# The last attention of a four-layer block: side work cut into smaller pieces over more steps, and its transfers in another order

## The chip, the cores and the metric

The kernel runs on one core of a Trainium2 chip. A core has five engines that each follow their own program: PE (matmuls, with PEld for the loading of weights), DVE (vector work), ACT (activations and copies), POOL (elementwise work on data outside PSUM) and SP, which here only issues DMA transfers. The metric is the device time of one execution in microseconds (us): 1222.36 us, the median of three runs (1219.72 to 1225.01).

## The reference

Four layers update `x` (4 sequences of 1024 tokens, 256 channels), each as `x + tanh(gate) * layer(layernorm(x))`: a cross-attention to 77 context tokens, a mixture of six experts, a second cross-attention with 16 heads, and a self-attention, which this text is about:

```python
qkv = (x @ W_qkv).reshape(Bx, Nx, 3, H, D)          # H = 16 heads of D = 16
q, k, v = (qkv[:, :, 0], qkv[:, :, 1], qkv[:, :, 2])
...
pos = sim > 0.9                                      # a class for each token but the first 5
logits = jnp.einsum('bqhd,bkhd->bhqk', q * scale, k)
...
x_pos = masked_attn(pos)                             # keys: the 5 registers and the tokens of pos
x_neg = masked_attn(~pos)                            # keys: the 5 registers and the others
reg_out = (x_pos[:, :REG] + x_neg[:, :REG]) * 0.5
tok_out = jnp.where(pos[:, :, None, None], x_pos[:, REG:], x_neg[:, REG:])
out = jnp.concatenate([reg_out, tok_out], axis=1).reshape(Bx, Nx, Cx)
return out @ W_proj + b_proj
```

A token attends to the registers and to its own class. The five registers (the first five tokens of a sequence) attend twice, once to each class, and take the mean.

## The kernel before

Three layers and the projections of the last one are laid out by a planner (class `Plan`, with costs and due times), which ends about 435 us into the span. The projections store the last layer's queries, keys and values in DRAM (`q_d`, `k_d`, `v_d`). The change touches almost only what follows.

**Units and steps.** The last attention works in 16 units: sequence `b` (4) by group `g` of four heads. A unit's queries and keys are fetched into a slot (`QT`, `KT`, four slots, reused every fourth unit) by `fetch` (L193, twelve DMAs of 128 KB, issued at L206); `classes` (L1473) adds four DMAs with rows that hold the class as large numbers. A unit takes 16 steps: two halves `ch` of the queries by eight tiles `t` of the keys. Step `k` is step `k % 16` of unit `k // 16`, so 256 steps in all, after 11 steps (`LEAD`) in which only maxima are made. In a step the loop at L1898 issues, in program order on PE, DVE and ACT:

- `scores` (L1678): for each of four heads a matmul (L1682, keys by queries, 512 columns) into a bank `sc`, and ACT's exp of it into `p` (L1690);
- between them `maxima` (L1638) for the unit 11 steps ahead: a matmul (L1647, queries by keys) into a bank `ps_m`, and DVE's maximum of it (L1654);
- `weigh` (L1694): the `p` of the step before times the values (L1700, eight instructions for four heads), into a bank `av`; ACT copies it to `part` (L1717) and POOL adds it to `raw` (L1718). Once no maxima are left, DVE adds it directly (L1712).

There are eight PSUM banks, taken in turn. `maxima_end` (L1656) turns eight tiles' maxima, and four small DMAs (L1670) write them as rows of `QT`; no score of that half of the unit may start before they have landed. They are issued at steps `16u - 3` and `16u + 5`, for use from `16u` and `16u + 8`.

**Side work.** The rest is written as generators. `plan(steps, gen)` (L1855) names the steps at whose end a generator goes on to its next `yield`:

- `registers(b)` (L1561): POOL prepares the registers' queries (32 small products, L1568 and L1569), PE makes their scores (L1577, two banks of 512 columns with eight matmuls each), ACT copies them to `p_r` (L1584), then maximum, exp, transposes (L1598), weighting (L1605) and the registers' result. It runs at steps `64b + 16` to `64b + 26`.
- `finish(b)` (L1730), for the sequence before: reciprocals of the softmax sums (L1735), the sums to DRAM (L1737), two fetches of 512 KB that spread them over the partitions (`rinv`, L1739 and L1743, one buffer), a product of 128x1024 on POOL after each (L1741, L1745), then four output tiles: eight passes of matmul into one bank (L1755), DVE's sum of 512 columns (L1757), a DMA of the result (L1758).
- `finish_unit`, `first_heads`, `divided` and `last_heads` do the same for the last sequence in parts; `biased(b)` (L1839) adds the bias to `X[b]` on POOL; `unit(u)` (L1843) fetches a unit; `fetch_values(b)` (L1465) fetches V; `values(b)` (L1488) makes V for sequences 2 and 3 in the first steps.

**Queues.** The program order of PE, DVE, ACT and POOL is kept as written (`manual_schedule`). SP isn't in that list: the builder's scheduler orders SP's DMAs by when it reckons their inputs ready, with program order as the priority. Each queue then runs in its order, and an instruction that waits holds those behind it.

## Time and profile before

| | us |
|---|---|
| median of the three runs | 1222.36 |
| the profiled execution | 1224.2 |
| its span, first to last instruction | 1222.2 |
| first step of maxima (L1647) | 435.8 |
| step 0 (first exp of L1690) | 472.9 |
| steps 16 / 64 / 128 / 192 | 521.3 / 648.3 / 833.7 / 1018.3 |
| end of the loop's last exp step (255) | about 1209 |

Over the span PE is busy 1153.5 us (94%), DVE 991.2 (81%), ACT 928.1 (76%), POOL 603.8 (49%). The mean granted clock of PE is 0.968 of full speed. The costliest groups are all of the last attention: DVE's 1024 maxima (L1654), 623.1 us; ACT's 1024 exps (L1690), 545.6; PE's matmuls of L1647, L1700 and L1682; POOL's 213 sums (L1718), 272.2.

How to read it: a step begins with the first of its four exps, so the distance between the first exps of two steps is the first one's length. The table of windows gives, for any stretch, how long each engine was busy in it. In a timeline, the bracket at a line's end says how long the engine stood idle before it and what ended that; "<-issue" means that the profile shows no cause. SP's lines are only the issuing of DMAs; the data lands later.

### The profile page before, as it was taken

The numbers are of one execution on the slowest core, as the hardware profiler recorded it, in microseconds if no ns is written. First come the engines' busy times: TensorE is split into PE (matmuls) and PEld (weight loads), VectorE is DVE, ScalarE is ACT, GpSimd is POOL, SyncE is SP. The second block draws the span as 40 slices with busy tenths as digits, with TensorE's granted clock in tenths as the row PEclk, the third lists the DMA queues.
The fourth block names the chain that finished last, engine by engine and source line by source line (L and its number), as shares of the span: only waits on it lengthen the run. The fifth ranks groups of instructions, "written<-read, shape, count | busy, mean of one in ns | idle before, by whom it ended". The sixth has DMA issues, their size and how long they took to land.

```text
span 1222.2 us, 25427 instructions
## 1 busy us (share of the span) xinstructions
PE 1153.5 (94%) x9100; PEld 609.7 (50%) x9100; DVE 991.2 (81%) x2057; ACT 928.1 (76%) x1910; POOL 603.8 (49%) x670
## 2 busy tenths in 40 slices
PE   7999999999999979999998899999899999799998
PEld 5666776777676554344333354333354333244333
DVE  6898686776864379979999779999779999678983
ACT  4865567776566314989998779999778999678985
POOL 6463566667757531545444435444445444345431
PEclk8998999999999978999999899999899999899999
DMA  8000021111112877522232323332423332310001
GB/s 234 23 1 12 13 71 63 44 42 47 55 44 98 239 190 169 93 49 46 49 57 56 85 68 59 50 57 47 92 56 64 54 60 41 64 33 22 20 20 36
DMA packets 58149, 80.08 MB, mean 66 GB/s; under 512 B 15845, under 2 KB 41360, under 8 KB 58022
## 3 DMA queue, kind: packets, MB, share of 16 engines
q1 hardware_dynamic: 56406, 77.17, 27.6%
q8 instruction: 72, 1.18, 0.4%
q10 hardware_dynamic: 1104, 1.04, 0.3%
q0 software_dynamic: 512, 0.25, 0.2%
q14 instruction: 55, 0.45, 0.1%
HBM read 47.39 MB, written 26.07 MB: 60 GB/s over the span
## 4 chain that ended last, share of the span: by engine, by line
PE 55%; DVE 29%; DMA 5%; ACT 4%; issue 3%; POOL 3%; SPq 1%; DVEq 0%; POOLq 0%; ACTq 0%
DVE nm L1654 21%; PE av L1700 12%; PE sc L1682 11%; PE ps_m L1647 4%; PE ps_st L1120 4%; PE ps_av L1132 2%; PE ps_o L1198 2%; PE ps_q L1233 2%; PE ps_o L1755 2%; PE ps_xt L780 2%; ACT p L1690 2%; PE ps_y L989 2%; PE ps_rs L1577 1%; DMA k_d<-stage 1%; DMA slot<-nmt 1%
## 5 line engine op out<-in xcount | busy, mean ns | idle before, releaser
L1654 DVE TENSOR_REDUCE nm<-ps_m 128x1 f32<-128x512 f32 x1024 | 623.1, 675 | 54.3 <-PE ps_m L1647 45.5
L1690 ACT ACTIVATE p<-sc 128x512 f32<-128x512 f32 x1024 | 545.6, 672 | 61.9 <-PE ps_m L1647 53.5
L1718 POOL TENSOR_TENSOR raw<-raw,part 128x512 f32<-128x512 f32 x213 | 272.2, 1278 | 384.2 <-ACT part L1717 377.5
L1647 PE MATMUL ps_m<-slot,slot 64*128 64x512 f32 x768 | 286.2, 456 | 0.7
L1700 PE MATMUL av<-p,v 128*32 128x512 f32 x2048 | 280.0, 616 | 1.0
L1682 PE MATMUL sc<-slot,slot 64*128 64x512 f32 x768 | 249.0, 438 | 8.1 <-DMA slot<-nmt 7.7
L1682 PEld LDWEIGHTS sc<-slot,slot 64*128 64x128 f32 x768 | 124.1, 185 | 182.1 <-DVE nm L1654 76.8
L1717 ACT COPY part<-av 128x512 f32<-128x512 f32 x213 | 138.7, 651 | 18.2 <-PE av L1700 17.0
L1647 PEld LDWEIGHTS ps_m<-slot,slot 64*128 64x128 f32 x768 | 130.5, 187 | 27.1 <-ACT p L1690 13.3
L1682 PE MATMUL sc<-qt,kt 64*128 64x512 f32 x256 | 89.1, 457 | 24.7 <-issue 15.4
L1279 POOL TENSOR_TENSOR ss_all<-ss_all,mhalf 128x16 f32<-128x16 f32 x32 | 92.6, 2902 | 12.8 <-DVE ss_all L1250 12.8
L1647 PE MATMUL ps_m<-kt,qt 64*128 64x512 f32 x256 | 92.4, 465 | 4.1 <-ACT vs L1499 2.4
L1682 PEld LDWEIGHTS sc<-qt,kt 64*128 64x128 f32 x256 | 45.9, 198 | 88.7 <-DVE nm L1654 38.8
L1700 PEld LDWEIGHTS av<-p,v 128*32 128x32 f32 x2048 | 41.2, 109 | 81.6 <-ACT p L1690 66.6
L1125 ACT ACTIVATE pt<-ps_st 77x512 f32<-77x512 f32 x128 | 64.1, 598 | 22.8 <-PE ps_st L1120 22.8
L1068 DVE TENSOR_REDUCE nm<-ps_e 128x4 f32<-128x308 f32 x128 | 51.7, 469 | 13.7 <-PE ps_e L1055 13.6
L768 ACT ACTIVATE xnp<-x,shift_all,rstd_all 128x256 f32<-128x256 f32 x96 | 52.0, 605 | 11.7 <-POOL shift_all L747 9.3
L735 DVE BATCH_NORM_STATS2 bn_st<-x 128x6 f32<-128x256 f32 x128 | 51.6, 403 | 2.4 <-DMA x<-in_x 1.9
L1647 PEld LDWEIGHTS ps_m<-kt,qt 64*128 64x128 f32 x256 | 42.5, 191 | 18.3 <-DVE nm L1654 4.9
L670 DVE TENSOR_TENSOR stage<-ps_s,stage 128x512 fp32r<-128x512 f32 x32 | 22.0, 690 | 25.3 <-ACT stage L237 25.1
L237 ACT COPY xt<-ps_xt 128x512 f32<-128x512 f32 (+1 forms) x57 | 31.7, 582 | 13.9 <-PE ps_xt L780 13.4
L744 POOL TENSOR_SCALAR rstd_all<-mv_all 128x2 f32<-128x2 f32 (+3 forms) x46 | 11.7, 254 | 61.2 <-DVE mv_all L736 49.6
(323 smaller groups left out, 1658.1 us busy)
## 6 DMA issues: line engine op xcount, KB each, us to landing
slot<-q_d SPq DMA_DIRECT2D x72, 128.0 KB
slot<-k_d SPq DMA_DIRECT2D x72, 128.0 KB
q_d<-stage SPq DMA_DIRECT2D x32, 256.0 KB
k_d<-stage SPq DMA_DIRECT2D x16, 512.0 KB
v_d<-vs SPq DMA_DIRECT2D x16, 272.0 KB
v<-v_d SPq DMA_DIRECT2D x16, 272.0 KB
x<-in_x SPq DMA_DIRECT2D x8, 512.0 KB
rin<-inv_d SPq DMA_DIRECT2D x32, 128.0 KB
```

The source lines that it names most:

```text
L735: ve.bn_stats(st[:, i, :], X[b][:, t0 + i, :])
L768: se.activation(to[:, i, :], xb[:, t0 + i, :], AF.Identity, bias=shift[:, i : i + 1], scale=rstd[:, i : i + 1],)
L1068: ve.tensor_reduce(g2["nm"][:, i, r], by_head, AX.X, ALU.max, negate=True)
L1125: se.activation(p[:, r], g2["st", c][r], AF.Exp)
L1279: gp.tensor_tensor(ss, ss, mhalf.to_broadcast([P, H]), ALU.pow)
L1647: pe.matmul(ps, QT[u % SLOTS][r, i, t * P : t * P + P], KT[u % SLOTS][r, i, h * CH : h * CH + CH], start=True, stop=True,)
L1654: ve.tensor_reduce(nm[:, 2 * i + j // 2, t % (T // 2), h : h + 1], ps, AX.X, ALU.max, negate=True)
L1682: pe.matmul(ps, KT[u % SLOTS][r, i, t * P : t * P + P], QT[u % SLOTS][r, i, ch * CH : ch * CH + CH], start=True, stop=True,)
L1690: se.activation(p[j], ps, AF.Exp)
L1700: pe.matmul(ps[32 * j : 32 * j + 32, :], V_all[b % 2][:, at : at + 32], p[j], start=True, stop=True)
L1717: se.copy(part, ps)
L1718: gp.tensor_tensor(to, to, part, ALU.add)
```

## The change

It touches the last attention and one store ahead of it.

- The generator `fetch` yields after each half of the queries and of the keys (three DMAs), `classes` after each of its two tensors. A unit's fetches are written at steps `16u - 42` to `16u - 39` (`16u - 34` to `16u - 31` for the first unit of a sequence), its classes at `+8, +9` (`+4, +5`) after the first; before, all stood at `16u - 40`. Unit 1 and the V of sequence 0 move from ahead of the loop into its first steps. V of the others is fetched in two pairs.
- Both stores of the class rows go out on ACT's queue.
- `plan` takes a step in brackets, `(k,)`: the generator then goes on in the middle of step `k`, after two of its four heads. `filled(k)` names the end of step `k` and the middle of step `k + 1`: matmuls are issued at the one, their bank is emptied at the other.
- The registers' scores take four banks of 256 columns instead of two of 512, one every second step, emptied in mid-step. The rest of `registers` follows a few steps later.
- The output tiles of `finish` cover 128 tokens instead of 256, one every third step from `64b + 97`, with DVE's sum in mid-step; before, they stood at `64b + 81` to `64b + 89`. `first_heads` is cut in the same way.
- `finish` fetches both `rinv` at step `64b + 74`, into two buffers; before, the first at 69 and the second at 74 into the same buffer.
- `biased` adds the bias in four parts. `finish_unit(0)` ends at step 226 instead of 219. `on` shares the three buffers of `part`.

```diff
     def fetch(u, q_rows, k_rows):
...
                     nc.sync.dma_start(out=dst[to : to + D].bitcast(F32), in_=heads[:, k])
+                yield
...
-                for s_, queue in enumerate((nc.sync, nc.scalar)):
-                    queue.dma_start(out=cls_d[s_].rearrange("k (t n) -> t k n", n=P), in_=r[:, s_])
+                for s_ in range(2):
+                    nc.scalar.dma_start(out=cls_d[s_].rearrange("k (t n) -> t k n", n=P), in_=r[:, s_])
...
         blank(1)
         gp.memset(V_all[0][:, NV:], 0.0)
-        fetch(1, QT[1], KT[1])
-        classes(1)
-        drain(fetch_values(0))
...
-        yield
-
-        p = work.tile([P, S], F32, name="p_r", tag="rinv", bufs=1)
-        for h in range(2):
-            ps = bank("ps_rs", [P, CH])
-            for n in range(2 * G):
-                g, i = divmod(n, 2)
+            if g % 2:
+                yield
+
+        p = work.tile([P, S], F32, name="p_r", tag="rinv", bufs=2)
+        n = CH // 2
+        for h in range(4):
+            ps = bank("ps_rs", [P, n])
+            for k in range(2 * G):
+                g, i = divmod(k, 2)
...
-            se.copy(p[:, h * CH : h * CH + CH], ps)
-        yield
+            yield
+            se.copy(p[:, h * n : h * n + n], ps)
+            yield
...
+        rinv = [work.tile([P, S], F32, name="rinv", tag="rinv", bufs=2) for e in range(2)]
+        for e in range(2):
+            nc.sync.dma_start(out=rinv[e], in_=bc(rinv_d[b][8 * e : 8 * e + 8], 1, D))
+        yield
+        for e in range(2):
+            gp.tensor_tensor(o[:, e, :], o[:, e, :], rinv[e], ALU.mult)
+            if e == 0:
                 yield
...
+        for t in range(T):
+            ps = bank("ps_o", [P, C])
+            for e in range(2):
+                pe.matmul(ps, o[:, e, t * P : t * P + P], w_proj[:, e, :], start=e == 0, stop=e == 1)
             yield
+            ve.scalar_tensor_tensor(x[:, t, :], ps, tg[:, 3:4], x[:, t, :], ALU.mult, ALU.add)
+            yield
+            if t % 2:
+                at = (t - 1) * P
+                nc.sync.dma_start(
+                    out=out[b, at : at + 2 * P].rearrange("(t p) c -> p t c", p=P), in_=x[:, t - 1 : t + 1, :]
+                )
+            yield
...
+        for t in range(T):
+            ps = bank("ps_o", [P, C])
+            pe.matmul(ps, o[:, 0, t * P : t * P + P], w_proj[:, 0, :], start=True, stop=True)
+            yield
+            ve.scalar_tensor_tensor(x[:, t, :], ps, tg[:, 3:4], x[:, t, :], ALU.mult, ALU.add)
             yield
...
-        on = work.tile([P, n, P], F32, name="on", bufs=2)
+        on = work.tile([P, n, P], F32, name="on", tag="part", bufs=3)
...
+        for t in range(0, T, 2):
+            x2 = X[b][:, t : t + 2, :]
+            gp.tensor_tensor(x2, x2, bc(b_proj, 1, 2), ALU.add)
+            yield
...
-            plan([k - 24, k - 22, k - 20, k - 18], fetch_values(b))
+        plan([k - 40, k - 38, k - 16, k - 14] if b else [-5, -4, -2, -1], fetch_values(b))
+        scored = [filled(k + n) for n in (17, 19, 21, 23)]
+        plan([k + 14, k + 15, *chain(*scored), k + 25, k + 26, k + 27, k + 29, k + 30, k + 31], registers(b))
+        plan([k + 27, k + 28, k + 35, k + 36], biased(b))
+        if b < B - 1:
+            tiles = chain(*([n, (n + 1,), n + 2] for n in range(k + 64 + 33, k + 64 + 55, 3)))
+            plan([k + 67, k + 68, k + 74, k + 78, k + 80, *tiles], finish(b))
         else:
-            plan([k + 19, k + 27], finish_unit(0))
+            plan([k + 19, k + 34], finish_unit(0))
             plan([k + 35, k + 39], finish_unit(1))
-            plan([k + 43, k + 45, k + 47, k + 49], first_heads())
+            plan(chain(*(filled(k + n) for n in (41, 42, 43, 45, 46, 47, 49, 50))), first_heads())
+    for u in range(1, NU):
+        at = {1: -11, 2: -1}.get(u, 16 * u - (42 if u % G else 34))
+        plan([at, at + 1, at + 2, at + 3], rows_ := unit(u))
+        plan({1: [-7, -6], 2: [3, 4]}.get(u, [at + 8, at + 9] if u % G else [at + 4, at + 5]), rows_)
...
                 maxima(um, km, [(j + 2) % J])
+                if j == 1:
+                    for gen in middle.pop(k, []):
+                        next(gen, None)
```

## The prediction

> **What bounds the kernel now.** I began with the page's slices of the span, then cut the last attention (435.8 us to the end) into its units with a table of windows, and then followed the two bad kinds of unit in the timelines.
>
> ```profile
> DVE  6898686776864379979999779999779999678983
> ACT  4865567776566314989998779999778999678985
> ```
>
> From slice 16 on, DVE and ACT stand at 9 together, with dips that return every fifth or sixth slice. In the windows the columns are stretch, its length, then busy time (and count) of PE, PEld, DVE, ACT and POOL, the granted clock, the DMA engines' share and GB/s.
>
> ```profile
> 521.30:568.80 47.50, 47.23 (x358) 21.21 (x358) 41.69 (x74) 43.01 (x87) 22.98 (x30) 0.96 0.29 49
> 608.50:648.30 39.80, 39.73 (x262) 15.54 (x258) 39.66 (x71) 39.40 (x81) 17.89 (x14) 1.00 0.30 51
> 648.30:698.60 50.30, 42.43 (x262) 16.98 (x258) 40.74 (x73) 40.03 (x81) 20.18 (x15) 0.90 0.35 66
> 668.00:676.00 8.00, 0.55 (x6) 0.19 (x2) 1.68 (x3) 1.08 (x2) 1.26 (x1) 0.74 0.91 130
> 676.00:681.00 5.00, 4.62 (x20) 2.07 (x22) 2.20 (x4) 2.45 (x5) 0.26 (x1) 0.50 0.44 92
> 698.60:754.00 55.40, 54.72 (x390) 26.49 (x386) 44.91 (x80) 43.81 (x87) 26.24 (x33) 1.00 0.33 73
> 1068.20:1126.40 58.20, 55.65 (x390) 26.32 (x386) 46.48 (x80) 44.52 (x87) 29.18 (x36) 1.00 0.10 29
> ```
>
> A quiet unit of 16 steps (608.5) takes 39.8 us, with DVE and ACT both busy for over 39 of it: 2.45 us a step in the mean, 2.39 in the shortest. So whatever adds work to DVE or ACT, or holds PE long enough to starve them, is paid. The other units are longer for two reasons. In 648.3 (steps 64 to 79) DVE and ACT have no more work than in the quiet unit; they wait. In 698.6 (steps 80 to 95) there is real work: 128 more matmuls.
>
> **The wait.** SP's timeline around step 72 (start, length of the issues, line):
>
> ```profile
> 663.88 0.34 SPq L1737 DMA_DIRECT2D rinv_d<-sums  x1
> 664.32 1.84 SPq L1670 DMA_DIRECT2D qt<-nmt  x3
> 666.27 0.63 SPq L1739 DMA_DIRECT2D rinv<-rinv_d  x1
> 666.95 0.53 SPq L1670 DMA_DIRECT2D qt<-nmt  x1
> ...
> 667.97 8.23 SPq L206 DMA_DIRECT2D slot<-k_d  x6
> 676.30 2.23 SPq L1479 DMA_DIRECT2D slot<-cls_d  x4
> 689.82 0.64 SPq L1743 DMA_DIRECT2D rinv<-rinv_d  x1
> ```
>
> The fourth `nmt` row, without which no score of step 72 may start, goes out behind a `rinv` fetch of 512 KB, and the fetches of unit 7 follow at once. PE takes up the scores only at 676.38, after 7.83 us of waiting; the first exp of step 73 starts 11.98 us after that of step 72. Steps 136 and 200 repeat it with 11.76 and 12.10. Afterwards PE runs at half clock for 5 us (the window 676). The three units with this wait (50.3, 49.6, 49.9) exceed 39.8 by 30.4 us in all. The waits of SP's queue say the same from its side, and that the second `rinv` fetch held it once more, because its only buffer had to be multiplied out first:
>
> ```profile
> SPq L1743 <- POOL o L1741: 10.9, 1, 10.9
> ...
> SPq L206 <- DMA rinv<-rinv_d: 5.6, 1, 5.6
> ```
>
> A smaller wait of this kind stands at step 16: unit 3's fetches and classes are issued from 503.2 to 514.8, `nmt` from 515.64, and PE waits 5.03 us. Steps 15 and 16 take 6.38 and 3.82 (clock 0.66 again) in place of 2.45 each: 5.3 us.
>
> **The change, part by part.** All terms are against the profiled execution: 1224.2 us, of which the span is 1222.2; the median of the runs shown is 1.8 lower.
>
> Order of the transfers. The reciprocals come at steps 67 and 68, and the `rinv` transfers move to step 74, both into buffers of their own: behind the `nmt` of step 69, ahead of that of step 77, which step 80 needs. From 74 to 80 there are six steps, 14.7 us. By then must have landed: the rest of unit 7's fetches (12 of 128 KB, now from step 70; at the 130 GB/s of the window 668:676 they take 12 us from step 70, so until 75), the 64 KB of `rinv_d`, then 1 MB of `rinv`, about 8 us at that rate: to step 79. It fits, barely. I count 27 of the 30.4 us as gained, leaving about 1 us a place for what is late next: `nmt` behind `rinv` at step 80, or POOL's first product at 78 (2.38 us) with eight small register products of 0.2 us beside it; POOL is half idle in the quiet unit (17.89 of 39.8), and three `part` buffers cover some two steps. Unit 3's fetches move from step 8 to 6 to 9 and its classes behind the `nmt` of 13: 4.5 of 5.3 us. Both class stores on ACT's queue: one issue more of 0.35 us where ACT waits 3.17 us; nothing. The earlier fetches of unit 1 and of V move past the stores of `vs`, while DVE reduces without a gap from 450.6 to 465: nothing, with 3 us either way.
>
> The price of a small insert. `ps_ra` and today's tile give it:
>
> ```profile
> 549.74 1.08 PE L1605 MATMUL ps_ra<-v,pt_r 128*32 128x64 f32 x64
> ...
> 551.27 1.09 ACT L1690 ACTIVATE p<-sc 128x512 f32<-128x512 f32 x2 [0.52 <-PE ps_m L1647]
> ...
> 715.97 0.75 DVE L1757 SCALAR_TENSOR_TENSOR x<-ps_o,tg,x 128x512 f32<-128x512 f32 x1 [1.22 <-PE ps_o L1755]
> ```
>
> `ps_ra` delays the next score by 0.97 us (549.77 to 550.74); ACT idles 0.52, DVE is not the one that suffers, and the step costs 0.74 more than 2.39. An output tile of today (eight passes from 713.93, the next score at 715.86) delays it by 1.93: ACT idles 1.56, DVE 1.22, since its sum is queued ahead of the reductions and PE has not finished. So the first half microsecond is hidden by work in the banks, and the rest is paid.
>
> Registers' scores. Today 16 matmuls of 512 columns at 0.233 us hold PE from 529.18 to 533.09, DVE idles 3.72, the step takes 6.20: 3.8 us a batch. After: four pieces of eight matmuls with 256 columns. The trace has no such matmul. From below it is half of 0.233, so 0.93 us a piece (the transposes at 541.33 show weights changed every 0.11 us, so loading does not forbid it); from above the full 0.233, 1.86 a piece. I take 0.93, nearest to `ps_ra`. ACT pays 0.52 for it and about 0.28 for the copy of 256 columns (512 cost 0.48 from start to start), now emptied between two exps so that it waits for nothing: 0.8 a piece, 3.2 a batch, a gain of 0.6, in four batches 2.4. Bounds: 0.3 a piece (only the copy) and 1.7.
>
> Output tiles. The unit 698.6 exceeds the quiet one by 15.6; the register work alone costs 6.3 (47.5 of unit 521.3, less 39.8, less 1.4 of clock after step 16), so four tiles cost 9.3. In unit 1068.2 it is 18.4 less 6.3, 12.1, with about 1.5 of `finish_unit`. After: eight tiles with four passes of 0.217 (0.87), and a DVE sum of 256 columns, about 0.75 less 0.27 of columns, some 0.41 from start to start, after two reductions. Bounds 0.41 (DVE alone) and 1.0 (the doubled `first_heads` tiles of today, four passes and a wide sum, cost 0.9 to 1.3 at steps 235 to 241). I take 0.7, next to `ps_ra`'s 0.74: 5.6 a batch. Gains 3.7, 3.7 and 5.0: 12.4. They no longer share steps with the registers, so POOL's wait at step 81 goes too.
>
> `first_heads`: four tiles at 4.1 today, eight of two passes at 0.45: gain 0.5. The bias in pieces of 1.28 us in place of 4.57 on POOL, and the third `on` buffer: nothing, as POOL has room.
>
> Sum: 27 + 4.5 + 2.4 + 12.4 + 0.5 = 46.8; 1224.2 - 46.8 = 1177.
>
> The rule that speaks against it. In the unit 698.6 the clock stayed at 1.00 among inserts and waits up to 2 us. The Trainium skill, "TensorE: Matmul & The Clock Gate", section "A second HAM failure mode: psum-queue depth-cycling", warns that short idles between groups of matmuls that cycle through PSUM banks make the clock fall back and recover. By the page, if each of the 48 new pieces cost one window of 3.4 us at half speed, that would be an estimated 82 us, and the change a loss. The measured 1.00 speaks against it here, and the sum goes by the row.
>
> **The rivals.** (1) The wait moves: `nmt` of steps 77, 141, 205 lands behind both `rinv`, 4 to 5 us late each; for it, the tight count above and that one `rinv` with fetches beside it took until 676; 1191. (2) The change doesn't do what it says. SP's queue isn't in program order: the four V fetches of the second batch, written at steps 40 to 46, are issued at 494.01, in step 6. If the builder draws both `rinv` forward to step 69, ahead of `nmt`, the wait stays whole: 1177 + 27 = 1204. (3) Slower: a bank held from the step's end to the next step's middle leaves seven for the pipeline. PE waits for banks all the time (115.6 us of the scores' idle is for DVE's reductions). If each of the 48 pieces then costs two reductions of 0.6 beside its 0.93 and 0.28, 2.4 us, that is 115 us against the 48 of today's blocks: with the 31.5 of waits gone, 1224 + 35 = 1259. It decides from 1.7 us a piece; `ps_ra` with 0.74 in one bank speaks against.
>
> **Numbers.** Forecast 0.66, (1) 0.13, (2) 0.11, (3) 0.06; 0.04 that the parts cancel. The range runs from 1162, with the pieces near their lower bounds (tiles at 0.41, scores at 0.3: 15 us better), to 1204. Half a per cent, about 6 us, is what a measurement can tell: faster 0.90, same 0.04, slower 0.06.
>
> **What to look for.** Step 72 near 2.5 us with no wait for `nmt`, no half clock after it; steps 15 and 16 the same. A step with a piece near 3.1. Wrong would be a score that waits for `nmt` at step 80, ACT's `part` waiting for POOL at 79 to 82, or pieces above 1.2 us.

## The result, and the profile after

The change makes no gain: 1226.74 us, the median of 20 runs (1222.08 to 1231.06), beside 1222.96 for the kernel before on the same chip (20 runs, 1218.99 to 1225.98). The ratio is 1.0033, 95% interval 1.0020 to 1.0045: slower, by less than half a per cent. The profiled execution took 1226.41, its span 1224.7. The forecast was 1177.

The slices of the span, DVE and ACT, as shown of before:

```profile
DVE  5898786776864489889999699999689899689884
ACT  4766567876566327899999698899699899689676
```

The dips are still there: each now reaches 6 (before, two of the three stood at 7), and they have moved a little. The windows say where to. Columns as before: stretch, length, busy time (and count) of PE, PEld, DVE, ACT and POOL, granted clock, DMA share, GB/s.

```profile
599.40:639.20 39.80, 39.74 (x262) 15.54 (x258) 39.66 (x71) 39.42 (x82) 17.92 (x14) 1.00 0.39 65
639.20:681.70 42.50, 41.61 (x256) 15.90 (x254) 41.46 (x73) 40.00 (x81) 17.91 (x14) 1.00 0.34 52
681.70:738.60 56.90, 48.25 (x372) 23.07 (x373) 42.30 (x75) 43.42 (x90) 28.45 (x36) 0.94 0.29 60
738.60:784.50 45.90, 45.85 (x282) 18.56 (x279) 42.20 (x77) 40.49 (x80) 20.38 (x16) 1.00 0.33 58
1117.10:1173.70 56.60, 52.38 (x292) 22.25 (x291) 49.66 (x83) 41.52 (x82) 26.01 (x23) 0.94 0.08 21
...
671.00:677.00 6.00, 5.99 (x40) 2.88 (x40) 5.93 (x13) 6.00 (x13) 2.72 (x3) 1.00 0.01 1
680.00:688.00 8.00, 1.50 (x10) 0.34 (x10) 2.44 (x5) 2.40 (x5) 3.19 (x3) 0.90 0.50 127
```

The first row is a quiet unit, as long as before. Unit 4 (639.2) has lost its wait: 42.5 instead of 50.3. Unit 5 (681.7) has got one: PE is busy for 48.25 of 56.90, and in 680 to 688 nearly every engine stands while 127 GB/s come in. From 671 to 677 the DMA engines were idle. SP's timeline says why:

```profile
655.64 2.39 SPq L1672 DMA_DIRECT2D qt<-nmt  x4
658.08 2.26 SPq L206 DMA_DIRECT2D slot<-q_d  x5
660.38 3.43 SPq L206 DMA_DIRECT2D slot<-k_d  x6
664.53 0.34 SPq L1738 DMA_DIRECT2D rinv_d<-sums  x1
676.77 1.72 SPq L1672 DMA_DIRECT2D slot<-nmt  x3
678.59 1.33 SPq L1741 DMA_DIRECT2D rinv<-rinv_d  x2
679.97 0.56 SPq L1672 DMA_DIRECT2D slot<-nmt  x1
```

`rinv_d` went out at 664.5, and nothing followed for 12 us. In the queue's order both `rinv` stand behind three of the four `nmt` (the small DMAs of `maxima_end`) of step 77, though the program writes them at step 74; those `nmt` can't go out before DVE has made them, at 676.8. The fourth `nmt` then lies behind 1 MB. It is the picture of before, eight steps later and with twice the bytes. PE's timeline, and the page's group of score matmuls, before and after:

```profile
690.11 0.76 PE L1684 MATMUL sc<-slot,slot 64*128 64x512 f32 x1 [8.62 <-DMA slot<-nmt]
```

```profile
L1682 PE MATMUL sc<-slot,slot 64*128 64x512 f32 x768 | 249.0, 438 | 8.1 <-DMA slot<-nmt 7.7
L1684 PE MATMUL sc<-slot,slot 64*128 64x512 f32 x768 | 248.3, 440 | 29.8 <-DMA slot<-nmt 28.7
```

The span by stretches (starts of steps are first exps), so that the difference of 2.5 us is accounted for:

| stretch | before | after | difference |
|---|---|---|---|
| up to step 0 | 472.9 | 466.8 | -6.1 |
| unit 0 (steps 15 and 16: 10.2, then 8.1) | 48.4 | 44.5 | -4.0 |
| units 1, 2, 3 | 127.1 | 127.9 | +0.9 |
| units 4, 8, 12: steps 72, 136, 200 | 35.8 | 8.3 | -27.6 |
| the same units, other steps | 114.0 | 119.5 | +5.5 |
| units 5, 9, 13: steps 80, 144, 208 | 7.2 | 37.9 | +30.7 |
| the same units, other steps (tiles gone) | 161.8 | 134.0 | -27.8 |
| units 6, 7, 10, 11 (tiles come) | 159.3 | 178.3 | +19.0 |
| unit 14 | 44.7 | 56.6 | +11.9 |
| unit 15 and the end | 51.0 | 51.0 | 0 |

### The profile page after: what moved, and what is told of

It reads as the page before. It is cut to its first block, busy times and chain, and to the rows that moved or that the text cites. A ratio compares the mean times of both kernels' runs of the same rounds, so it can differ in the third digit from the quotient of the medians.

```text
span 1224.7 us, 25560 instructions
## 1 busy us (share of the span) xinstructions
PE 1157.0 (94%) x9164; PEld 611.3 (50%) x9164; DVE 999.4 (82%) x2073; ACT 932.1 (76%) x1918; POOL 607.0 (50%) x682
## 4 chain that ended last, share of the span: by engine, by line
PE 75%; DVE 11%; DMA 5%; ACT 4%; POOL 2%; issue 1%; SPq 0%; ACTq 0%; DVEq 0%; POOLq 0%
PE av L1702 20%; PE sc L1684 18%; PE ps_m L1649 8%; DVE nm L1656 5%; PE ps_st L1121 4%; DMA slot<-nmt 3%; PE ps_av L1133 2%; PE ps_o L1199 2%; PE ps_o L1755 2%; PE ps_q L1234 2%; PE ps_xt L781 2%; PE ps_y L990 2%; PE ps_rs L1578 1%; ACT p L1692 1%; PE ps_xb L886 1%
## 5 line engine op out<-in xcount | busy, mean ns | idle before, releaser
L1684 PE MATMUL sc<-slot,slot 64*128 64x512 f32 x768 | 248.3, 440 | 29.8 <-DMA slot<-nmt 28.7
L1684 PEld LDWEIGHTS sc<-qt,kt 64*128 64x128 f32 x256 | 43.0, 186 | 67.7 <-DVE nm L1656 31.4
L746 POOL TENSOR_TENSOR rstd_all<-rstd_all,mhalf 128x2 f32<-128x2 f32 (+3 forms) x46 | 39.5, 858 | 3.8
```

The lines of the kernel that those rows point to most:

```text
L1684: pe.matmul(ps, KT[u % SLOTS][r, i, t * P : t * P + P], QT[u % SLOTS][r, i, ch * CH : ch * CH + CH], start=True, stop=True,)
```

## The experiments

All times are medians beside runs of the kernel before on the same chip (1220.7 to 1221.0 in these comparisons), so the ratio to before is what compares them; after itself stands at 1.0033. L numbers are those of each kernel.

| run | us | ratio to before, 95% |
|---|---|---|
| rinv_step72 | 1202.24 | 0.9846 (0.9826 to 0.9866) |
| rinv_step70 | 1200.24 | 0.9833 (0.9812 to 0.9854) |
| rinv_late | 1207.93 | 0.9893 (0.9870 to 0.9916) |
| empty_at_once | 1211.88 | 0.9931 (0.9911 to 0.9950) |
| tiles_whole | 1224.41 | 1.0024 (1.0007 to 1.0041) |
| scores_whole | 1224.66 | 1.0034 (1.0020 to 1.0048) |
| bias_early | 1221.94 | 1.0010 (0.9994 to 1.0026) |
| recip_apart | 1226.07 | 1.0043 (1.0028 to 1.0057) |
| recip_later | 1223.41 | 1.0013 (0.9995 to 1.0031) |
| early_fetch | 1224.77 | 1.0036 (1.0021 to 1.0051) |
| before_late | 1198.80 | 0.9818 (0.9798 to 0.9838) |
| all_mended | 1192.81 | 0.9773 (0.9736 to 0.9810) |
| mended_step70 | 1182.37 | 0.9682 (0.9647 to 0.9717) |
| mended_step71 | 1199.69 | 0.9837 (0.9795 to 0.9879) |

**The place of the 1 MB in SP's queue.** My theory after the result: the order alone costs 30 us. The rival: the bytes don't fit between the two `nmt` in any order.

```diff
-            plan([k + 67, k + 68, k + 74, k + 78, k + 80, *tiles], finish(b))
+            plan([k + 67, k + 68, k + 72, k + 78, k + 80, *tiles], finish(b))
```

> The kernel after with one number changed: the three transfers of a finished batch (rinv_d, two rinv) are issued at step 72 of their unit instead of 74. In the order of SP's queue both rinv then stand ahead of all four nmt of step 77, with one k_d fetch between rinv_d and rinv and five k_d fetches behind. Theory (order in the queue): after lost 9.9 us at each of steps 80, 144 and 208 because the 1 MB started only behind three nmt that are issued at step 77, 7 to 8 us after rinv_d had landed; now it starts at about step 74, the nmt follow the fetches, and steps 80/144/208 fall from 12.4, 12.5 and 13.0 us to about 2.6: minus 30 us, 1197. Rival (the bytes): 1 MB and twelve fetches do not fit between step 70 and step 80 on the 16 engines in any order; the five k_d pushed behind the 1 MB hold the nmt, and step 80 stays 4 to 6 us too long, in all minus 12 to 18 us, 1209 to 1215. Second rival (the wait goes back to step 72): SP stands before rinv until rinv_d has landed and what is behind it comes late; then a wait of some us at step 72 to 76 or at unit 6's first step, and no gain.

SP's timeline of this run:

```profile
658.09 0.42 SPq L1738 DMA_DIRECT2D rinv_d<-sums  x1
658.56 0.43 SPq L206 DMA_DIRECT2D slot<-k_d  x1
663.28 1.34 SPq L1741 DMA_DIRECT2D rinv<-rinv_d  x2
664.68 2.32 SPq L206 DMA_DIRECT2D slot<-k_d  x5
674.48 4.83 SPq L1672 DMA_DIRECT2D slot<-nmt  x4
```

Two steps earlier in the program, and the 1 MB starts 15.3 us earlier (663.28 instead of 678.59; 13.0 counted from the start of step 72), ahead of all four `nmt`. The ratio falls from 1.0033 to 0.9846, some 23 us. It is not 30: steps 79 to 81 still sum to 13.0, 11.8 and 9.9 in place of some 8. SP's waits show why. It stood before `rinv` for some 4 us a batch until `rinv_d` had landed:

```profile
SPq L1741 <- DMA rinv_d<-sums: 12.5, 3, 4.3
```

And of the four `nmt`, which DVE had made by 674.8, the third went out only at 677.86, when the second `rinv` had landed; so the four took 4.83 us to issue instead of some 2.3. With step 70:

```diff
-            plan([k + 67, k + 68, k + 74, k + 78, k + 80, *tiles], finish(b))
+            plan([k + 67, k + 68, k + 70, k + 78, k + 80, *tiles], finish(b))
```

> The kernel after with the three transfers of a finished batch issued at step 70 of their unit instead of 74: rinv_d ahead of the first q_d fetch, both rinv behind the four nmt of step 69 and ahead of the other eleven fetches. With the transfers at step 72 the profile showed rinv waiting in SP's queue from 659.0 to 663.3 us for rinv_d, the DMA engines nearly idle from 662.3 to 665, both rinv and the fetches done at about 682, and the score of step 80 3.5, 2.4 and 1.5 us late in the three batches, with another 0.3 to 1.2 us in the step after. Theory (order in SP's queue and one idle stretch; the bytes themselves fit between steps 70 and 80): without the idle stretch the same bytes end 4 to 5 us sooner, the four nmt of step 77 land in time, steps 79 and 80 (143 and 144, 207 and 208) are 2.4 to 2.6, and the kernel is 8 to 10 us under the one with step 72, 1193. Rival (the bytes): the engines that carry the 1 MB are the last in either order, the nmt still land at about 683 and the time stays at 1202. Second rival: the 1 MB ahead of the fetches makes classes or maxima of the unit to come late, and steps 84 to 96 grow.

```profile
655.37 0.35 SPq L1738 DMA_DIRECT2D rinv_d<-sums  x1
655.82 0.36 SPq L206 DMA_DIRECT2D slot<-q_d  x1
658.88 2.33 SPq L1672 DMA_DIRECT2D qt<-nmt  x4
661.32 1.33 SPq L1741 DMA_DIRECT2D rinv<-rinv_d  x2
662.70 2.39 SPq L206 DMA_DIRECT2D slot<-q_d  x5
665.13 13.08 SPq L206 DMA_DIRECT2D slot<-k_d  x6
679.75 2.34 SPq L1672 DMA_DIRECT2D slot<-nmt  x4
```

Now `rinv_d` lands while SP waits for `nmt`, and the wait at step 80 is gone but for some 0.4 us at step 80 and 1.2 us ahead of step 208 (steps 80, 144, 208: 2.78, 2.41, 2.54; step 207: 3.55). So the bytes fit: the theory holds for these steps, and what was left with the transfers at step 72 came from the pause. Steps 81, 145 and 209 now take 4.36, 4.77 and 3.47 (3.33, 4.04 and 3.34 in after). Of the run's waits around step 81, the first line below, and then POOL's timeline:

```profile
PEld ps_rs L1578 <- POOL qr L1568: 0.8, 3, 0.3
```

```profile
683.82 2.37 POOL L1744 TENSOR_TENSOR o<-o,rinv 128x1024 f32<-128x1024 f32 x1
...
690.53 0.20 POOL L1567 TENSOR_TENSOR qr<-slot,rmul 128x10 fp32r<-128x10 f32 x1
690.82 0.20 POOL L1568 TENSOR_TENSOR qr<-qr,radd 128x10 fp32r<-128x10 f32 x1
```

That is the next thing late: the first piece of the registers' scores waits for their queries, which POOL makes behind its product. Units 4, 5, 8, 9, 12 and 13 are 27.7 us shorter than in after, 21.1 with step 72. The 8 to 10 us that I expected on top of step 72 don't show in the time: the medians differ by 2 us, within their intervals. In this run's one profile the lead-in and unit 0, which the edit doesn't touch, took 5 us more; whether its other executions share that isn't known.

The third place: behind everything, with a third `rinv` buffer (and two buffers instead of three for the values of the lead-in, to make room).

```diff
-        rinv = [work.tile([P, S], F32, name="rinv", tag="rinv", bufs=2) for e in range(2)]
+        yield
+        rinv = [work.tile([P, S], F32, name="rinv", tag="rinv", bufs=3) for e in range(2)]
...
-            plan([k + 67, k + 68, k + 74, k + 78, k + 80, *tiles], finish(b))
+            plan([k + 67, k + 68, k + 74, k + 80, k + 85, k + 87, *tiles], finish(b))
```

> The kernel after with the 1 MB moved behind everything that the next unit's start waits for: rinv_d issued at step 74 as in after, both rinv at step 80 in a step of their own, behind the nmt of step 77 and the class rows, the two multiplications at steps 85 and 87 instead of 78 and 80. For that the rinv buffers are three instead of two, and the lead-in's values have two buffers instead of three. Theory (order in SP's queue, and room between step 80 and the next fetches at step 94): no wait at steps 72, 79, 80 or 81, each 2.4 to 2.5 (81: 3.3, with its piece), minus 30 us, 1195. Rival (the 1 MB beside the sums and the o rows of step 80, or POOL's multiplications in steps 85 to 92, make something late there): steps 85 to 93 longer by 3 us or more a batch, 1204 or above.

The wait at 80 is gone in all three places (2.39 each), but steps 83, 147 and 211 take 5.2 and steps 215 and 216 6.6 and 3.9. The rival was right that something behind step 80 would be late and on the time, but not on the place. For the second of these losses the queue of SP shows how:

```profile
1056.69 0.34 SPq L1772 DMA_DIRECT2D rinv_d<-sums  x1
1064.11 0.56 SPq L1672 DMA_DIRECT2D slot<-nmt  x1
1067.14 0.55 SPq L1776 DMA_DIRECT2D rinv<-rinv_d  x1
1067.78 1.74 SPq L1672 DMA_DIRECT2D slot<-nmt  x3
```

The builder has again put a `rinv` (that of `finish_unit(0)`) among the four `nmt`, and this one had to wait for a buffer until POOL's product of step 213 ended at 1067.11. What makes step 83 long was not found; PE waits there for banks that DVE empties.

**The price of a piece.**

```diff
                 pe.matmul(ps, o[:, e, t * P : t * P + P], w_proj[:, e, :], start=e == 0, stop=e == 1)
-            yield
             ve.scalar_tensor_tensor(x[:, t, :], ps, tg[:, 3:4], x[:, t, :], ALU.mult, ALU.add)
             yield
...
-        scored = [filled(k + n) for n in (17, 19, 21, 23)]
+        scored = [[k + n] for n in (17, 19, 21, 23)]
...
```

(The first edit stands for the three places in which the `yield` between matmuls and emptying goes; the plans of the tiles and of `first_heads` lose their mid-steps as `scored` does.)

> The kernel after with every piece (registers' scores, output tiles, first heads) emptied at the end of the step that computes it instead of in the middle of the next; sizes, steps and order of the pieces stay. Theory (mid-step emptying buys nothing: the price of a piece is the time of the engine that empties it, 0.81 us on DVE or 0.5 on ACT, which comes on top in either place): step with a piece about 3.4, the next about 2.6, sum as now, 1226 within 4 us. Rival (emptying at the end of the step makes the tensor engine wait for the bank, or stands ahead of the next step's first work): each of the 48 pieces 0.5 us dearer, 1250. Second rival (emptying in mid-step pushes the maxima's reductions back and keeps banks from PE): each piece 0.3 us or more cheaper, 1212.

The second rival was right: 1% faster than after, 15.7 us less span for 48 pieces. DVE's timelines around the first output tile, after and then this run:

```profile
740.40 3.07 DVE L1656 TENSOR_REDUCE nm<-ps_m 128x1 f32<-128x512 f32 x5
744.28 1.29 DVE L1656 TENSOR_REDUCE nm<-ps_m 128x1 f32<-128x512 f32 x2 [0.81 <-PE ps_m L1649]
745.49 0.48 DVE L1757 SCALAR_TENSOR_TENSOR x<-ps_o,tg,x 128x256 f32<-128x256 f32 x1
```

```profile
736.86 3.67 DVE L1655 TENSOR_REDUCE nm<-ps_m 128x1 f32<-128x512 f32 x6
740.95 0.48 DVE L1755 SCALAR_TENSOR_TENSOR x<-ps_o,tg,x 128x256 f32<-128x256 f32 x1 [0.43 <-PE ps_o L1754]
741.35 5.46 DVE L1655 TENSOR_REDUCE nm<-ps_m 128x1 f32<-128x512 f32 x9
```

While PE makes the piece (1.06 us, 742.66 to 743.72 in after), DVE runs dry. Emptied at once, the sum fills that hole; emptied in mid-step, it comes after two more reductions, and the hole stays. The step with the piece is as long either way (3.29 and 3.30), the one behind it 2.75 in after and 2.39 here. That is 0.36 a piece, and 48 of them make 17 us.

```diff
+        for t in range(0, T, 2):
+            ps = bank("ps_o", [P, 2, C])
...
-            tiles = chain(*([n, (n + 1,), n + 2] for n in range(k + 64 + 33, k + 64 + 55, 3)))
+            tiles = [k + 64 + n for n in (33, 39, 45, 51)]
...
```

> The kernel after with the output product of batches 0 to 2 in four tiles of 256 tokens, each computed, emptied and stored at the end of one step (33, 39, 45 and 51 steps behind its unit 4's start), instead of eight tiles of 128 tokens emptied in mid-step; the last batch's first heads stay in pieces. In after eight pieces cost 9.5 us a batch in batches 0 and 1 (units 6 and 7 are 46.0 and 43.2 beside 39.7 and 39.8); in before four whole tiles cost 9.3, beside other work in the same unit. Theory (the price is DVE's: 0.81 us of emptying a piece, in steps in which DVE has no room, so that pieces and whole tiles cost the same DVE time): four whole tiles cost 8.5 to 10 us a batch here too, and the time is the same within 3 us, 1224 to 1229. Rival (each insertion has a price of its own, whatever its size): four cost 5 us, minus 12 us or more in three batches, 1214. Second rival (pieces are cheaper, as the prediction had it): whole tiles cost 13 us or more, 1237.

The theory was right, narrowly: units 6 and 7 are 46.0 and 42.3 long, 8.7 us over two quiet ones, against 9.5 with eight pieces in after and 7.4 (44.6 and 42.4) with eight pieces emptied at once. Halving the tile gains nothing by itself.

```diff
-        n = CH // 2
-        for h in range(4):
-            ps = bank("ps_rs", [P, n])
+        for h in range(2):
+            ps = bank("ps_rs", [P, CH])
...
-        plan([k + 14, k + 15, *chain(*scored), k + 25, ...
+        plan([k + 14, k + 15, k + 18, k + 25, ...
```

> The kernel after with the registers' scores of a batch in two tiles of 512 keys in one step, emptied at its end, as before the change, instead of four tiles of 256 in four steps emptied in mid-step; the rest of after stays. In after the four pieces cost 1.3 us each, 5.2 us a batch (steps 17, 19, 21, 23 of 3.3 and the steps behind them of 2.75, beside 2.40). Theory (each insertion into a full step has a price of its own, whatever its size): whole they cost the 3.8 us that the profile of before shows, 1.4 us a batch less, minus 5 to 6 us, 1221. Rival (the price goes with the matmul time, and the pieces' 5.2 us have another cause, such as the fetches that run in the same steps): no change within 2 us, 1226.

The time is unchanged, as the rival said. Unit 1 takes 47.2 instead of 48.3, units 5 and 9 (without step 80 or 144) 43.7 and 43.7 instead of 44.4 and 45.1, while unit 13 (without step 208) takes 45.6 instead of 44.4: in three of four batches whole is about 1 us cheaper than four pieces emptied in mid-step, less than I had for it.

**DVE held by POOL.**

```diff
-        plan([k + 27, k + 28, k + 35, k + 36], biased(b))
+        plan([k + n for n in ((27, 28, 35, 36) if b < B - 1 else (21, 22, 23, 24))], biased(b))
```

> The kernel after with the last batch's four bias pieces on POOL at steps 213 to 216 instead of 219, 220, 227 and 228; nothing else. Theory (DVE's small nm<-nm of step 228 waits until POOL's run without a gap ends: product of step 226, two small ones, part, bias, part, bias, part): the run is two pieces of 1.2 us shorter and has gaps, the operation of 4.49 us falls to under 1 us, steps 229 to 231 (6.51, 4.67, 3.98) to about 3.0 each, minus 6 us, 1221. Rival (the long steps are those of the tiles and the first heads' pieces, and the 4.49 us are only where DVE happened to stand): no change, 1227, with the same 6.5 us somewhere in steps 228 to 231.

After's DVE at step 228, and POOL beside it:

```profile
1131.61 4.49 DVE L1663 TENSOR_TENSOR nm<-nm 128x16 f32<-128x16 f32 x1
```

```profile
1129.88 1.27 POOL L1720 TENSOR_TENSOR raw<-raw,part 128x512 f32<-128x512 f32 x1
1131.11 1.27 POOL L1843 TENSOR_TENSOR x<-x,b_proj 128x512 f32<-128x512 f32 x1
1132.35 1.27 POOL L1720 TENSOR_TENSOR raw<-raw,part 128x512 f32<-128x512 f32 x1
1133.58 1.25 POOL L1843 TENSOR_TENSOR x<-x,b_proj 128x512 f32<-128x512 f32 x1
1134.80 1.25 POOL L1720 TENSOR_TENSOR raw<-raw,part 128x512 f32<-128x512 f32 x1
```

With the bias elsewhere, DVE and POOL of the run:

```profile
1131.47 0.93 DVE L1663 TENSOR_TENSOR nm<-nm 128x16 f32<-128x16 f32 x1
```

```profile
1129.74 2.63 POOL L1720 TENSOR_TENSOR raw<-raw,part 128x512 f32<-128x512 f32 x2
1134.13 1.28 POOL L1720 TENSOR_TENSOR raw<-raw,part 128x512 f32<-128x512 f32 x1 [1.77 <-ACT part L1719]
```

An elementwise minimum of two sets of 16 columns, 0.17 us elsewhere, ends when POOL's unbroken run ends, at 1136.05 in after and at 1132.37 here. Of the 32 `nm<-nm` of the last attention in after, the 20 that begin with POOL idle all take 0.17 to 0.18 us; all that take longer begin while POOL is at work and end within 0.04 us of the end of a POOL instruction. Steps 229 to 231 fall from 15.2 to 10.0 us. The ratio falls from 1.0033 to 1.0010, with intervals that just touch. The theory holds, and the steps show it better than the time.

**The reciprocals.** In after steps 69 to 72 take 3.49, 3.50, 3.25, 2.75; a quiet unit has 2.5, 2.8, 2.4, 2.4 there.

```diff
-            plan([k + 67, k + 68, k + 74, k + 78, k + 80, *tiles], finish(b))
+            plan([k + 67, k + 69, k + 74, k + 78, k + 80, *tiles], finish(b))
```

> The kernel after with the second half of a batch's reciprocal at step 69 instead of 68, so that one step lies between the two halves, as before the change. Theory (the two halves in adjacent steps, 0.53 us each, put DVE behind, and the ring of banks stays in a bad phase): steps 69 to 71 (133 to 135, 197 to 199) fall from 3.49, 3.50, 3.25 to about 2.6, in three places some 2.5 us each, minus 7 to 8 us, 1219. Rival (the steps are long because nm<-nm, which takes 0.97 instead of 0.17 us there, waits for POOL, or because of the fetches): no change of those steps, 1226.

My theory fell: 3.50, 3.30, 3.30, 2.75, and no time gained. Then, further away:

```diff
-            plan([k + 67, k + 68, k + 74, k + 78, k + 80, *tiles], finish(b))
+            plan([k + 71, k + 73, k + 74, k + 78, k + 80, *tiles], finish(b))
```

> The kernel after with the two reciprocals of a batch at steps 71 and 73 of their unit instead of 67 and 68; the transfers stay at step 74, so that the wait at step 80 stays as in after or grows by 1 us. With the halves one step apart (67 and 69) steps 69 to 72 had stayed 3.50, 3.30, 3.30, 2.75. Theory (what makes these steps long is that 1.06 us of DVE work stand ahead of the nmt of step 69 on a DVE with no room, and that the wait at step 72, in which DVE caught up before the change, is gone): steps 69 to 72 fall to about 2.5, 2.8, 2.4, 2.4, the 1.06 us appear behind step 71, about minus 1.5 us a batch, 1222. Rival (the price moves along whole, as DVE does not catch up wherever the reciprocals stand): steps 71 to 76 grow by 2.9 us a batch, 1226.

Steps 69 to 72 are those of a quiet unit (2.51, 2.81, 2.39, 2.39), and from 73 to 79 six steps have grown by 0.3 to 0.4: 41.8 us a unit instead of 42.6, with 39.8 in a quiet one. Both were half right. DVE's 1.06 us are paid two to three times over. That ends without a stall: in after step 73 is back at 2.39, and in before_late (below), which has the reciprocals at the same steps as this run and no wait at step 80, steps 80 and 81 are back at 2.49 and 2.39. What decides how long it lasts was not found. Before the change the wait at step 72 came in between, and little of the price showed: steps 69 to 71 took 2.57, 2.82, 2.82.

**The early fetches.**

```diff
         gp.memset(V_all[0][:, NV:], 0.0)
+        drain(fetch(1, QT[1], KT[1]))
+        drain(classes(1))
+        drain(fetch_values(0))
...
-    for u in range(1, NU):
-        at = {1: -11, 2: -1}.get(u, 16 * u - (42 if u % G else 34))
+    for u in range(2, NU):
+        at = {2: -1}.get(u, 16 * u - (42 if u % G else 34))
...
```

> The kernel after with unit 1's rows, its class rows and the first batch's values fetched ahead of the loop, as before the change, instead of in pieces at steps -11 to -1; all else as in after. In after step 0 started 6.1 us sooner than in before (466.8 beside 472.9) and step 15 took 4.8 instead of 6.4. Theory (those gains come from these fetches alone, which held the DMAs of unit 0 and of the lead-in): step 0 at 472 to 473, units 0 and 1 as in before but for the pieces, plus 6 to 10 us, 1233 to 1236. Rival (the gain at step 0 comes from something else, such as the class rows stored by ACT's queue alone or first_values in pieces): step 0 stays at 467 and the time at 1226.

The rival was right: step 0 stays early (464.6). Steps 15 and 16 lose their wait altogether (2.38, 2.39), steps 0 to 2 get 2.3 us longer, and unit 0 is as long as in after. In thirteen profiles of kernels that come from after, step 0 starts between 464.4 and 470.4, in all_mended at 472.1; in before and before_late it starts at 472.9 and 474.3. What this hangs on was not found.

**One part alone, and all parts mended.** before_late is the kernel before with only `finish` moved and cut anew, and the buffers that this takes:

```diff
-            plan([k + 67, k + 69, k + 74, k + 79, k + 81, k + 83, k + 87, k + 89], finish(b))
+            plan([k + 71, k + 73, k + 76, k + 80, k + 85, k + 87, k + 64 + 33, k + 64 + 39, k + 64 + 45, k + 64 + 51], finish(b))
```

> The kernel before with one part of the change alone, put where no wait is expected: three rinv buffers, reciprocals at steps 71 and 73, rinv_d at 76, both rinv at 80, the multiplications at 85 and 87, and the four whole output tiles at steps 97, 103, 109 and 115. Fetches, registers' scores, bias and first heads stay as in before. (The lead-in's values have two buffers instead of three.) Theory (of the whole change only the end of the waits behind rinv gains): steps 72, 136 and 200 fall from 12.0 to 2.5, minus 28 us, with 1 us less a batch for tiles that stand alone, 1192 to 1196. Rival (before's wait at step 72 covered DVE's lag and fetches that are late anyway): the gain is under 20 us, 1205.

It gains 22 us, nearer to the theory. Steps 72, 136 and 200 are 2.39, which is 28.7 us less. Of what is lost against that, 4.3 us lie in the other steps of units 4, 8 and 12, which carry the reciprocals, and 3.1 in steps 215 and 216 (7.4 and 4.9; 4.6 and 4.5 in before).

all_mended is the kernel after with these edits in one, and with the edits of rinv_late, empty_at_once and early_fetch that aren't printed again:

```diff
-            plan([k + 67, k + 68, k + 74, k + 78, k + 80, *tiles], finish(b))
+            plan([k + 71, k + 73, k + 76, k + 80, k + 85, k + 87, *tiles], finish(b))
...
-        scored = [filled(k + n) for n in (17, 19, 21, 23)]
+        scored = [[k + n] for n in (17, 19, 21, 23)]
...
-        plan([k + 27, k + 28, k + 35, k + 36], biased(b))
+        plan([k + n for n in ((27, 28, 35, 36) if b < B - 1 else (21, 22, 23, 24))], biased(b))
...
+        drain(fetch(1, QT[1], KT[1]))
...
```

> The kernel after with all that the runs so far gave: rinv at step 80 behind nmt and class rows (three buffers), reciprocals at 71 and 73, rinv_d at 76, multiplications at 85 and 87, every piece emptied at the end of its own step, the last batch's bias at steps 213 to 216, unit 1's rows and the first values ahead of the loop. Theory (the gains are of different stretches and add up: 30 for rinv, 15 for emptying at once, 5 for the bias, 1.5 for the early fetch, 0 to 4 for the reciprocals): 1226 less 51 to 56, 1170 to 1175. Rival (some of the stalls covered others, as the wait at step 72 covered DVE's lag): 1180 to 1190.

It took 1192.8, outside both: the losses of rinv_late (steps 83, 147 and 211 with 5.2, and 215 with 7.2) came with it. So the last pair is without the third `rinv` buffer and has the transfers back at step 70 (first line), or at 71 with the reciprocals one step sooner (second line):

```diff
+            plan([k + 67, k + 68, k + 70, k + 78, k + 80, *tiles], finish(b))
...
+            plan([k + 66, k + 67, k + 71, k + 78, k + 80, *tiles], finish(b))
```

> As all_mended, but with the 1 MB as in rinv_step70: two rinv buffers, the transfers at step 70 ahead of the fetches, reciprocals at 67 and 68 and multiplications at 78 and 80 as in after. In all_mended 18 to 20 us of the hoped sum were missing: step 83 of 5.2 us (2.1 too long, in three batches), steps 215 and 216 of 7.2 and 4.0 us, and 472 instead of 465 us up to step 0. Theory (those losses belong to the 1 MB at step 80, which collides with the nmt and the multiplications of the following half, and the other gains add up): minus 26 for rinv (as rinv_step70), 15, 5 and 1.5 from 1226, 1178 to 1181. Rival (stalls cover one another; whatever place the 1 MB has, the same 15 us turn up elsewhere): 1190 or more.

> As mended_step70, with the reciprocals at steps 66 and 67 and the transfers at step 71, behind the third and fourth of the q_d fetches. Theory (the 2.9 us of steps 69 to 72 come from DVE's 1.06 us so shortly ahead of the maxima's end at step 68 and the nmt at step 69, on a DVE with no room; with one step more between them they are paid in plain steps, 0.35 us each): steps 67 to 72 sum to 1 us less a batch, the time 3 us lower than with the reciprocals at 67 and 68, if the 1 MB at step 71 doesn't hold nmt at step 80; 1176. Rival (the lag lasts until a stall, wherever it begins): the same sum or more, 1179 to 1183.

mended_step70 is 3.2% faster than before, the fastest of all. The parts add up: alone, rinv_step70, empty_at_once, bias_early and early_fetch move the ratio from 1.0033 by -0.0200, -0.0102, -0.0023 and +0.0003, together to 0.9711; measured 0.9682 (0.9647 to 0.9717). mended_step71, with two things moved at once, was slower than that instead of faster. Its units 4, 8 and 12 take 49.8, 50.0 and 46.8 instead of 43.1, 42.8 and 42.4 in mended_step70, its steps 68 and 69 alone 6.75 and 5.91. Windows of it:

```profile
645.00:649.00 4.00, 3.79 (x17) 1.12 (x16) 4.00 (x9) 3.83 (x8) 2.43 (x2) 1.00 0.38 82
649.00:659.00 10.00, 9.28 (x29) 2.57 (x29) 4.27 (x8) 3.90 (x7) 1.27 (x1) 0.51 0.00 1
659.00:663.00 4.00, 3.35 (x19) 1.13 (x19) 2.98 (x6) 2.73 (x6) 1.27 (x1) 0.95 0.09 19
```

For 10 us PE runs at 0.51 of its clock, with 29 matmuls instead of some 66. PE had idled 0.2 us (until 648.98) before the clock fell and 0.7 (until 650.29) as it fell, and the DMA engines were idle; what set it off, and which of the two moves it belongs to, was not settled.

## Why the prediction was wrong

**The step that failed** is "behind the `nmt` of step 69, ahead of that of step 77", the premise of "It fits, barely". I had the place where the program writes the 1 MB, and took it for the place in SP's queue, although my own fence of before showed a `rinv` drawn in between three `nmt` and the fourth. I counted the bytes from step 74 on; they started behind step 77. The byte count itself was good: some 20 us were forecast for 1 MB and twelve fetches, and rinv_step70, which has the 1 MB and eleven fetches between the same two `nmt`, though the 1 MB first, loses only 1.2 us to them in one place and 0.4 in another. At steps 72, 136 and 200, 27.6 us went, as forecast; at 80, 144 and 208, 30.7 came. The sign of being wrong that I had named, a score that waits for `nmt` at step 80, is the one that was seen.

**Rival 1** named mechanism and place. Its price, 4 to 5 us a place, supposed that the 1 MB was under way by step 74; behind the `nmt` it costs 10. Rival 2 knew that the builder reorders SP, and looked for `rinv` only too early, not too late.

**What was late next.** I named `nmt` and POOL's first product beside the registers' small ones; the latter came out as said, about 1 us a place (steps 81 and 145 of rinv_step70). DVE I left out: its 1.06 us of reciprocals had largely been covered by the stall, and units 4, 8 and 12 lost 5.5 us in their other steps once it was gone.

**The price of a small insert**, 0.7 to 0.8, was mis-sized: 1.2 to 1.3 as built, 0.9 to 1.0 emptied at once. A piece holds PE for longer than I had: 1.06 us instead of 0.87 for a tile, 1.14 instead of 0.93 for the registers' scores (695.80 to 696.94 of after). PE's time is paid nearly whole; the half microsecond "hidden by work in the banks" isn't there. That the emptying "waits for nothing" in mid-step was wrong: it misses DVE's idle moment. The tiles' move gained 27.8 us in units 5, 9 and 13 and cost 19.0 in units 6, 7, 10 and 11, and most of what is left of unit 14's 11.9 after the bias: a few us, not 12.4. The registers' scores lost about 1 us in three of four batches instead of gaining 0.6 in each. Rival 3's point, 1.7 us, was not reached. In after's units 6, 7, 10 and 11, which have pieces and no stall, the clock is 1.00, as I had weighed it; in unit 14 it falls (0.94) behind DVE's 4.49 us. A quiet unit's mean step is 2.49 us (39.8 over 16), not the 2.45 that I gave; that changes nothing here.

**"Nothing, as POOL has room"** was wrong in the last batch, by 5.2 us: room over a unit isn't room at the moment when DVE needs to get in.

**Steps 15 and 16** gave 2.1 of 4.5. Up to step 0, 6.1 came that I hadn't in the sum; their cause is open.

## What to carry to other kernels

Where a scheduler orders a queue, take the order from the queue's own timeline: a large transfer with an input still under way is put behind small ones that can't go yet, and what stands behind it pays for the whole. Before you take a stall away, list what hides in it, on every engine. Put the emptying of a bank where its engine runs dry, which is right behind the matmuls that starved it.

## What the runs showed of the hardware

- A DVE operation on two SBUF tensors waits for POOL: `nm<-nm` takes 0.17 us alone, up to 1.07 against the rest of one POOL sum (0.93 to 0.97 in most of the steps named here), 4.49 against the rest of one and three more. The Trainium skill, "SBUF — State Buffer", section "Who interferes with whom", states the rule behind it: a DVE instruction with two SBUF inputs contends with a GpSimd instruction that reads SBUF, over ports that they share under an exclusive lock. The trace agrees, and goes further: DVE didn't get in between POOL's instructions, which followed one another without a gap.
- The two `rinv` fetches keep the DMA share at 0.50 with 127 GB/s (680 to 688 of after), the fetches of 128 KB keep it at 1.05 with 156 (657 to 662 of rinv_step72). The Trainium skill, "DMA: Bandwidth & Descriptors", section "Why a DMA increments its semaphore by 16 and not by 1", says that the slowest dimensions of a transfer's two sides set how many of the 16 engines it uses, the largest number up to 16 that divides both; on the DRAM side of `rinv` that dimension is 8, which agrees with a share of one half. Whether 16 would be faster was not tried.
- In these kernels a large transfer on SP's queue also holds what stands eight places behind it. Six `k_d` fetches were issued in 3.4 us in after and in 13.1 in rinv_step70: the second and third of them went out at 670.63 and 676.09, each when the `rinv` eight places ahead of it had landed, though they don't use it. The third `nmt` of rinv_step72 stands eight places behind the second `rinv` in the same way. Whether the program or the queue sets the eight, no run shows. SP's waits in rinv_step70:

```profile
SPq L206 <- DMA rinv<-rinv_d: 31.2, 6, 5.7
```

- The clock fell to 0.51 for 10 us in mended_step71 without any long wait before it. The Trainium skill, "TensorE: Matmul & The Clock Gate", section "A second HAM failure mode: psum-queue depth-cycling", tells of such a fall after short idles between groups of matmuls. After's 48 pieces set off no such fall; this run has what looks like it, in three places.
